# A whole-kernel list scheduler, mask copies on ScalarE and softmax sums on VectorE in a cross-attention and windowed-attention network

## The chip, the cores and the metric

The kernel runs on one NeuronCore of a Trainium2 chip. The core has TensorE (PE, matrix products), VectorE (DVE), ScalarE (ACT), GpSimd (POOL) and SyncE (SP, which issues most DMAs). Each engine works through its own queue in order; semaphores make one wait for another. The metric is the time of one execution on the device, in microseconds (us), as the median of several runs. Less is better.

## The reference

The input x has 32 batch elements of 128 tokens with 128 features, in float32. First comes one cross attention to a context of the same shape (16 query heads, 4 key heads of width 8, a time bias, a mask), then six layers of windowed self attention and feed forward:

```python
x = x + xattn(layernorm(x), ctx, ctx, deltas, mask, Wq, Wk, Wv, Wo, tw)
y = layernorm(x)
for i in range(6):
    s = shift_tokens(y)                      # second half of the features: one token later
    q, k, v = split(s @ Wqkv[i], 3)          # 16 heads of width 64
    q, k = l2norm(q) * qs, l2norm(k) * ksc   # then rotary tables cos, sin and a scale
    sim = 8 * q @ k.T                        # windows of 32: each looks at itself and the one before
    y = softmax(masked(sim)) @ v @ Wo[i] + y
    s = layer_norm(shift_tokens(y)) * g + bln
    a, gate = split(s @ W1[i] + b1[i], 2)    # 341 + 341 columns
    y = (a * gelu(gate)) @ W2[i] + b2[i] + y
return x + y
```

## The kernel before

The work unit of the layers is one batch element of one layer: 6 x 32 = 192 units. Four units are a group (`GB`), which shares the input transposes (`ax`, `axh`, `axl`) and the feed forward. Cross attention likewise has 32 units in 8 groups, each with one softmax per key head (`attn_ops`).

A layer unit goes through these steps. `qk` projects queries and keys, four PSUM banks of 512 columns, each as three products of high and low float32r parts (`split3`). Of each bank, ScalarE takes the squares (`sq`), VectorE sums them per head (`ss`) and multiplies the bank with two rotary tables (`ta` and `tb`, line 694), and GpSimd adds the two halves (`add`). The reciprocal norms of all 32 heads come as Ln, then Exp with scale -0.5 on ScalarE, refined by one Newton step on VectorE (`rsqrt_a`, `rsqrt_b`, `rsqrt_c`, lines 116 to 137). GpSimd multiplies them in (`mul`), TensorE transposes (`tq`), and ScalarE copies queries and keys out of PSUM (`ev`, `ew`); one of the four half copies of keys is done by VectorE (line 744). `y` projects the values already multiplied with Wo, ScalarE copies them out (`yt`), and 16 DMAs regroup their windows (`dm`).

Scores are taken in two halves of eight heads. In each, a bfloat16 matmul of an identity with the mask (line 781) fills the bank, and the score matmuls add to it; VectorE takes the row maxima (`mx`); ScalarE takes eight exponentials of 64 columns, each with the sum of its row as an accumulator output (`ex`, line 804), which the profile shows as a second instruction, ACTIVATION_READ_ACCUMULATOR; then reciprocal (`rl`), product on GpSimd (`pl`), a 32x32 transpose on VectorE (`PT`) and the products with the values (`av`).

At the end of a group come residual and feed forward: `res`; one DMA of 127 rows that shifts half of the features by one token (`psh`); the statistics, their Ln and Exp; then `gate`, three Gelus (`gel`), `pa`, `um`, `w2`, `res2`. ScalarE evaluates functions from a table set that has to be loaded. The compiler puts a load where the set at hand lacks the function. The kernel itself asks for the set `natural_log_exp_and_others` at the start (line 140) and behind the last Gelu of each group (line 912).

The order on every engine is written out by hand: the tables `OFF1`, `GOFF1`, `OFF` and `GOFF` give each step of each unit a place in time, `push` puts it in a heap, and `drain` emits all in the order of these times. Buffers come from rotating pools. PSUM has five banks for projections, transposes and the like (`pj`), two for scores (`pscr`) and one for attention outputs (`pou`).

Of the kernel before, what the change touches and what calls it, by code (L numbers as in the profile page):

```python
# [16 lines left out]
P = 128  # L17
# [5 lines left out]
NRT = 8  # L23
NYT = 4
NKB = 3
NQT = 3
EWD = (1,)
STORE = 0.4
MP1 = [23.0 + 1.2 * i for i in range(8)]
WV1, DH1, DL1 = [20.85, 22.05], 0.15, 0.3  # L30
PREP0, PREPT = 10.0, 7.0
SHIFT = 6.0
FFT = 7.0
MP = [31.47, 31.72, 31.97, 32.22, 32.47, 32.72, 32.97, 33.22]
WV, BIAS, DH, DL = [24.4, 25.4], 16.4, 0.06, 0.14
T1 = 7.0
NI1 = 180
OFF1 = dict(
    sc=[[0, 2, 26, 28], [32, 34, 73, 75], [93, 95, 139, 141], [154, 159, 170, 172]],
    mx=[[1, 3, 27, 29], [33, 35, 74, 76], [94, 96, 140, 142], [158, 164, 171, 173]],  # L40
    sb=[[4, 5, 30, 31], [36, 37, 77, 78], [97, 98, 143, 144], [165, 168, 174, 175]],
    ex=[[39, 41, 44, 48], [99, 100, 101, 102], [151, 152, 155, 160], [187, 189, 192, 196]],
    tp=[[42, 46, 51, 55], [126, 127, 128, 129], [153, 157, 163, 167], [190, 194, 199, 203]],
    st=[[45, 50, 54, 57], [130, 132, 134, 135], [156, 162, 178, 179], [193, 198, 202, 205]],
    pa=[[49, 53, 82, 83], [131, 133, 136, 137], [161, 166, 186, 188], [197, 201, 218, 220]],
    oT=[[84], [138], [191], [223]], pb=[[145], [146], [195], [227]], rl=[[147], [148], [200], [232]],
    at=[[149], [150], [204], [236]],
)
GOFF1 = dict(
    ldc=[-101], gst=[-121, -120], gr0=[-119], gr1=[-117, -116], gr2=[-115, -114, -113], xa=[-118], xb=[-112],  # L50
    px=[-89], pxe=[-88], pcx=[-100], pce=[-99], pk=[-77], ke=[-76], kd=[-75], pq=[-74, -73, -71, -67],
    qe=[-72, -69, -65, -62], qd=[-70, -66, -63, -60], pv=[-55], vt=[-11], td=[-110], ab=[-109, -108], ln=[-4],
    mkb=[-56], tbm=[-3], p2=[238], aT=[249], pw=[265], rs=[266], hst=[267, 268], hr0=[269], hr1=[292, 296],
    hr2=[299, 301, 302], xf1=[270], xf2=[303],
)
T = 13.3
NI = 331
OFF = dict(
    qk=[[0, 1, 30, 31], [79, 80, 107, 108], [153, 154, 194, 195], [244, 245, 284, 285]],
    sq=[[2, 6, 32, 36], [81, 85, 109, 113], [155, 159, 196, 200], [246, 250, 286, 290]],  # L60
    ss=[[7, 11, 37, 41], [86, 90, 114, 118], [160, 164, 201, 205], [251, 255, 291, 295]],
    ta=[[3, 8, 33, 38], [82, 87, 110, 115], [156, 161, 197, 202], [247, 252, 287, 292]],
    tb=[[4, 9, 34, 39], [83, 88, 111, 116], [157, 162, 198, 203], [248, 253, 288, 293]],
    add=[[5, 10, 35, 40], [84, 89, 112, 117], [158, 163, 199, 204], [249, 254, 289, 294]],
    rs0=[[42], [119], [206], [296]], rs1=[[62, 63], [141, 142], [219, 220], [313, 314]],
    rs2=[[64, 65, 66], [143, 144, 145], [221, 222, 223], [315, 316, 317]],
    mul=[[67, 68, 69, 70], [146, 147, 148, 149], [224, 225, 226, 227], [318, 319, 320, 321]],
    tq=[[100, 102, 104, 136], [181, 183, 185, 228], [268, 270, 272, 275], [354, 356, 358, 381]],
    ev=[[101, 103, 105, 137], [182, 184, 186, 229], [269, 271, 273, 276], [355, 357, 359, 382]],
    ew=[[106, 138], [187, 230], [274, 277], [360, 383]],  # L70
    y=[[127, 128, 131, 150], [235, 236, 239, 281], [304, 305, 308, 328], [374, 375, 376, 407]],
    yt=[[129, 132, 134, 151], [237, 240, 242, 282], [306, 309, 311, 329], [384, 386, 388, 408]],
    dm=[[130, 133, 135, 152], [238, 241, 243, 283], [307, 310, 312, 330], [385, 387, 389, 409]],
    sc=[[124, 125, 178, 179], [216, 217, 260, 261], [301, 302, 347, 348], [390, 391, 426, 427]],
    mx=[[126, 180], [218, 262], [303, 349], [392, 428]],
    ex=[[165, 166, 212, 213], [256, 257, 297, 298], [343, 344, 377, 378], [422, 423, 451, 452]],
    rl=[[167, 214], [258, 299], [345, 379], [424, 453]], pl=[[168, 215], [259, 300], [346, 380], [425, 454]],
    PT=[[231, 232], [322, 323], [402, 403], [470, 471]], av=[[263, 264], [350, 351], [429, 430], [506, 507]],
)
GOFF = dict(  # L80
    ax=[-53], axh=[-52], axl=[-51], res=[508], psh=[564], fst=[565, 596], xn1p=[598], frs0=[597], frs1=[655, 656],
    frs2=[657, 658, 683], xn2p=[684], ptn=[735], xnh=[736], xnl=[737], gate=[831, 832, 833], gel=[834, 835, 836],
    pa=[850, 851, 853], um=[852, 854, 855], w2=[869, 870, 871, 872], res2=[873],
)

@with_exitstack
def body(ctx: ExitStack, tc: tile.TileContext, x, ctx_in, fside, mask, xWq, xWk, xWv, xWo, xtw,
# [5 lines left out]
    NG = B // GB  # L93
    HC = [(0, 128), (128, 128), (256, HID - 256)]
    RT = HC[2][1]

    const = ctx.enter_context(tc.tile_pool(name="const", bufs=1))
    small = ctx.enter_context(tc.tile_pool(name="small", bufs=4))

    nC = cst.shape[1] - 512  # L100
    cs = const.tile([P, nC], F32, tag="cs", name="cs")
# [5 lines left out]
    shift = cs[:, 516:644]  # L107
    identb = const.tile([P, P], BF16, tag="identb", name="identb")
    nc.vector.tensor_copy(identb, ident)
    maskb = const.tile([P, 512], BF16, tag="maskb", name="maskb")  # L110
    xt = const.tile([P, B, P], F32, tag="xt", name="xt")

    def rsqrt_a(src, n, eps, floor, tagp):
        v = small.tile([P, n], F32, tag=tagp + "v", name=tagp + "v")
        if eps is not None:
            nc.vector.tensor_scalar(v, src, eps, None, op0=ALU.add)
        else:
            nc.vector.tensor_scalar(v, src, floor, None, op0=ALU.max)  # L118
        y = small.tile([P, n], F32, tag=tagp + "y", name=tagp + "y")
        t = small.tile([P, n], F32, tag=tagp + "t", name=tagp + "t")  # L120
        return v, y, t

    def rsqrt_b(a, c):
        v, y, t = a
        if c == 0:
            nc.scalar.activation(y, v, AF.Ln)
        else:
            nc.scalar.activation(y, y, AF.Exp, scale=-0.5)

    def rsqrt_c(a, c):  # L130
        v, y, t = a
        if c == 0:
            nc.vector.tensor_tensor(t, y, y, op=ALU.mult)
        elif c == 1:
            nc.vector.scalar_tensor_tensor(t, v, -0.5, t, op0=ALU.mult, op1=ALU.mult)
        else:
            nc.vector.scalar_tensor_tensor(y, t, 1.5, y, op0=ALU.add, op1=ALU.mult)  # L137
        return y

    nc.scalar.preload_act_table_set("natural_log_exp_and_others")  # L140

    wch = ctx.enter_context(tc.tile_pool(name="wch", bufs=1))
    wst = ctx.enter_context(tc.tile_pool(name="wst", bufs=1))
    pj = ctx.enter_context(tc.tile_pool(name="pj", bufs=5, space=PSUM))
    pscr = ctx.enter_context(tc.tile_pool(name="pscr", bufs=2, space=PSUM))
    pou = ctx.enter_context(tc.tile_pool(name="pou", bufs=1, space=PSUM))

    heap = []
    seq = [0]

    def push(t, fn, a):
        heapq.heappush(heap, (t, seq[0], fn, a))
        seq[0] += 1

    def drain():
        while heap:
            _, _, fn, a = heapq.heappop(heap)
            fn(*a)

    NU = NG * GB  # L160
    ws = [None] * (L + 1)

    def prep_ops(l):
        w = ws[l] = {"qk": [None] * 4, "m": [None] * 4}
        wqk = Wqkv[l]
        V = {}

        def ld(i):
            if i == 0:
                V["w1r"] = wst.tile([P, 2 * HID], F32, tag="stg", name="w1r", bufs=2)  # L170
                nc.sync.dma_start(V["w1r"], W1[l])
            elif i == 1:
                V["col"] = wst.tile([P, 2], F32, tag="lgb", name="lgb")
                nc.sync.dma_start(V["col"][:, 0:1], ln_g[l].unsqueeze(1))
            elif i == 2:
                nc.sync.dma_start(V["col"][:, 1:2], ln_b[l].unsqueeze(1))
            elif i == 3:
                w["b1"] = wch.tile([P, 2, 3], F32, tag="b1c", name="b1c", bufs=2)
                nc.vector.memset(w["b1"], 0.0)
                for s in range(2):  # L180
                    nc.sync.dma_start(w["b1"][:, s, 0:2],
                                      b1[l, s * HID:s * HID + 2 * P].rearrange("(i p) -> p i", p=P))
# [69 lines left out]
        def wve(c):  # L252
            if c == 0:
                V["wvT"] = wst.tile([P, 8, P], F32, tag="stg", name="wvT", bufs=2)
# [781 lines left out]
```

## Time and profile before

| | us |
|---|---|
| median of 3 runs | 3326.27 |
| lowest, highest | 3325.03, 3327.11 |
| span of the profiled execution | 3320.9 |

The span runs from the first to the last instruction of the profiled execution; the device time holds a little around it. These groups of the page are of use below. Each has line, engine, operation, tile written and tiles read, shapes, and count; then busy time in us and the mean length of one in ns; then the idle time of the engine just before them and what ended most of it.

```profile
L700 POOL TENSOR_TENSOR rt<-t,t 128x512 f32<-128x512 f32 x768 | 980.3, 1286 | 372.8 <-DVE t L694 330.8
L694 DVE TENSOR_TENSOR t<-pqk,tab 128x512 f32<-128x512 f32 x1536 | 983.3, 681 | 115.9 <-ACT sq L686 110.3
L804 ACT ACTIVATE pr<-sc,mx 128x64 f32<-128x64 f32 x3072 | 915.7, 331 | 61.2 <-DVE PT L817 53.0
L804 ACT ACTIVATION_READ_ACCUMULATOR pr<-sc,mx 128x1 f32 x3072 | 691.9, 225 | 0.0
L689 DVE TENSOR_REDUCE ss<-sq 128x8 f32<-128x512 f32 x768 | 517.4, 674 | 0.0
```

The lengths of neighbours overlap: an instruction may start before the end of the one ahead of it on the same engine. So the time that an instruction takes up is better read from its start to the next start, in a timeline.

### The profile page before, as it was taken

To read this page: it belongs to the slowest core of one execution; us is meant where nothing else is said; L and a number is where in the kernel's file an instruction comes from. 1 tells how busy PE (TensorE), PEld (TensorE's weight loads), DVE (VectorE), ACT (ScalarE), POOL (GpSimd) and SP (SyncE) were. 2 spreads that over 40 slices of the span, in tenths; PEclk is the share of its full clock that TensorE was granted. 3 is DMA by queue.
4 is the path that set the end of the run, shared out by engine and by line. 5 is a ranking of instruction groups with operands and counts; after the bars stand their busy time and mean duration, and the time that the engine had idled before them with its cause. 6 is when DMAs were issued, how large, how long until landed. Compare 5 with 4: busy or idle time off the path is not lost.

```text
span 3320.9 us, 102077 instructions
## 1 busy us (share of the span) xinstructions
PE 3155.8 (95%) x35979; PEld 2389.3 (72%) x35979; DVE 2979.5 (90%) x6954; ACT 2834.9 (85%) x9983; POOL 2468.3 (74%) x2284
## 2 busy tenths in 40 slices
PE   8999899999999999999999999999999999999997
PEld 5555677777777777777777777777777777777775
DVE  6666899999999999999999998998999998999995
ACT  6776888898888898889898889898888898898895
POOL 5655777777787777787787787786787776777873
PEclk9999999999999999999999999999999999999998
DMA  2110333332333332233332333332333332333332
GB/s 61 33 37 12 77 87 82 79 74 71 75 83 86 78 74 72 72 85 84 77 77 71 75 83 81 79 77 68 79 83 76 84 76 64 77 82 81 82 83 62
DMA packets 217966, 243.80 MB, mean 73 GB/s; under 512 B 83534, under 2 KB 112498, under 8 KB 217458
## 3 DMA queue, kind: packets, MB, share of 16 engines
q1 hardware_dynamic: 217026, 236.93, 28.8%
q8 instruction: 288, 4.72, 0.6%
q14 instruction: 220, 1.80, 0.2%
q10 hardware_dynamic: 432, 0.34, 0.0%
HBM read 25.31 MB, written 4.19 MB: 9 GB/s over the span
## 4 chain that ended last, share of the span: by engine, by line
PE 49%; DVE 32%; ACT 8%; issue 4%; DMA 3%; SPq 2%; POOL 1%; ACTq 0%; DVEq 0%; POOLq 0%
DVE t L694 10%; PE pO L830 8%; PE ptq L729 7%; DVE ss L689 6%; PE sc L786 4%; DVE rnv L118 3%; PE pa L542 3%; PE pqk L636 3%; PE pqk L638 3%; ACT pr L804 3%; PE pqk L637 3%; DVE mx L793 2%; DVE PT L817 2%; SPq L769 2%; PE py L636 2%
## 5 line engine op out<-in xcount | busy, mean ns | idle before, releaser
L700 POOL TENSOR_TENSOR rt<-t,t 128x512 f32<-128x512 f32 x768 | 980.3, 1286 | 372.8 <-DVE t L694 330.8
L694 DVE TENSOR_TENSOR t<-pqk,tab 128x512 f32<-128x512 f32 x1536 | 983.3, 681 | 115.9 <-ACT sq L686 110.3
L804 ACT ACTIVATE pr<-sc,mx 128x64 f32<-128x64 f32 x3072 | 915.7, 331 | 61.2 <-DVE PT L817 53.0
L723 POOL TENSOR_TENSOR rt<-rt,rny 128x512 f32<-128x512 f32 x768 | 777.4, 1043 | 214.1 <-DVE rny L137 213.4
L804 ACT ACTIVATION_READ_ACCUMULATOR pr<-sc,mx 128x1 f32 x3072 | 691.9, 225 | 0.0
L689 DVE TENSOR_REDUCE ss<-sq 128x8 f32<-128x512 f32 x768 | 517.4, 674 | 0.0
L830 PE MATMUL pO<-ysh,PT 128*32 128x128 f32 x10752 | 416.9, 275 | 53.3 <-DVE PT L817 48.7
L813 POOL TENSOR_TENSOR pr<-pr,rl 128x512 f32<-128x512 f32 x384 | 400.8, 1044 | 89.2 <-DVE rl L809 89.2
L686 ACT ACTIVATE sq<-pqk 128x512 f32<-128x512 f32 x768 | 429.3, 600 | 24.6 <-PE pqk L638 12.5
L830 PEld LDWEIGHTS pO<-ysh,PT 128*32 128x32 f32 x10752 | 367.1, 110 | 97.6 <-DVE PT L817 72.1
L762 ACT COPY yt<-py 128x512 f32<-128x512 f32 x768 | 416.8, 614 | 21.2 <-PE py L638 17.2
L729 PE MATMUL ptq<-cs,rt 128*128 128x128 f32 x3072 | 409.8, 278 | 22.2 <-DVE t L694 17.0
L729 PEld LDWEIGHTS ptq<-cs,rt 128*128 128x128 f32 x3072 | 334.5, 141 | 96.7 <-issue 52.5
L786 PE MATMUL sc<-kb,qT 128*32 128x128 f32 (+1 forms) x12288 | 375.1, 262 | 15.2 <-DVE kb L744 14.8
L786 PEld LDWEIGHTS sc<-kb,qT 128*32 128x32 f32 x12288 | 270.7, 109 | 114.5 <-issue 70.7
L636 PE MATMUL py<-mw,xsh 128*128 128x512 f32 x768 | 333.1, 434 | 8.9 <-ACT yt L762 5.8
L636 PE MATMUL pqk<-wqh,xsh 128*128 128x512 f32 x768 | 314.0, 409 | 4.8 <-ACT yt L762 2.8
L638 PE MATMUL py<-mw,xsl 128*128 128x512 f32 x768 | 301.9, 393 | 0.0
L638 PE MATMUL pqk<-wqh,xsl 128*128 128x512 f32 x768 | 300.9, 392 | 0.0
L637 PE MATMUL pqk<-wql,xsh 128*128 128x512 f32 x768 | 300.8, 392 | 0.0
L637 PE MATMUL py<-mw,xsh 128*128 128x512 f32 x768 | 300.6, 391 | 0.0
L735 ACT COPY qT<-ptq 128x512 f32<-128x512 f32 x384 | 208.1, 590 | 79.0 <-PE ptq L729 78.1
(168 smaller groups left out, 5756.8 us busy)
## 6 DMA issues: line engine op xcount, KB each, us to landing
ysh<-yt SPq DMA_DIRECT2D x3072, 64.0 KB
raw<-in_L_ffn_Wqkv SPq DMA_DIRECT2D x36, 256.0 KB
xsu<-xt SPq DMA_DIRECT2D x48, 127.0 KB
wor<-in_L_ffn_Wo SPq DMA_DIRECT2D x6, 512.0 KB
xt<-in_x SPq DMA_DIRECT2D x8, 256.0 KB
cx<-in_ctx SPq DMA_DIRECT2D x8, 256.0 KB
mk<-in_mask_BxS_ff SPq DMA_DIRECT2D x8, 256.0 KB
x_scratch<-xt SPq DMA_DIRECT2D x8, 256.0 KB
```

The lines of the kernel that those rows point to most:

```text
L636: nc.tensor.matmul(pt, lh, rh, start=True, stop=False)
L637: nc.tensor.matmul(pt, lh, rl, start=False, stop=False)
L638: nc.tensor.matmul(pt, ll, rh, start=False, stop=True)
L686: nc.scalar.activation(V["sq", c], V["pp", c], AF.Square)
L689: nc.vector.tensor_reduce(V["ss"][:, c * 8:(c + 1) * 8], V["sq", c].rearrange("p (h d) -> p h d", d=64), axis=AX.X, op=ALU.add)
L694: nc.vector.tensor_tensor(V["t", k, c].rearrange("p h s d -> p h (s d)"), V["pp", c].rearrange("p (h d) -> p h d", d=64), w["tab"][:, c // ...
L700: nc.gpsimd.tensor_tensor(V["rt", c], V["t", 0, c], V["t", 1, c][:, :, ::-1, :], op=ALU.add)
L723: nc.gpsimd.tensor_tensor(rv, rv, V["rn"][:, c * 8:(c + 1) * 8].unsqueeze(2).to_broadcast([P, 8, 64]), op=ALU.mult)
L729: nc.tensor.transpose(V["ptq", c][:, k, :], V["rt", c][:, 2 * k:2 * k + 2].rearrange("p h s d -> p (h s d)"), ident)
L786: nc.tensor.matmul(sc[32 * c:32 * c + 32, :, wd, lo:64], qT[:, c, 32 * wd:32 * wd + 32], kT[:, c, :, 32 * wd - 32 + lo:32 * wd + 32], star ...
L804: nc.scalar.activation(pr[:, q, :], scv[:, q, :], AF.Exp, bias=mx[:, q:q + 1], accum_out=ls[:, q:q + 1])
L830: nc.tensor.matmul(pO[32 * wd:32 * wd + 32, j, :], PT[:, half, wd, blk, :], ysh[u][:, (2 * par + half) * P:(2 * par + half + 1) * P], star ...
```

## The change

The hand-written orders go. A class `Sched` takes every step of the whole kernel as an operation with an engine, a time it occupies the engine and a time until its result is there (the table `COST`), a priority (the place of its unit, moved by `LATER`), the buffers it reads and writes, and for some a table, "E" or "G". `run` then plays all engines forward and gives each free engine its first ready operation in order of priority for which buffers are free. What comes out is again a fixed order on each engine. A switch between "E" and "G" counts as 1.3 us more in the plan. Ln, both kinds of Exp and the softmax Exp are all "E"; Gelu is "G".

The steps change too:

- ScalarE copies the mask into the score bank (`msk`), in place of the matmul. There is one score bank, and `pj` has six.
- The exponentials keep their eight pieces per half, in two operations of four, without the accumulator output; VectorE sums the rows (`sm`).
- Both table products are one VectorE instruction over 1024 columns (`tab`).
- All Newton steps are on GpSimd (`newton`), five instructions where VectorE had four.
- ScalarE does all four half copies of keys (`evk`).
- x is kept with its shifted half beside it, in 192 columns. The shift is done after both residuals, each time as two DMAs, of 112 and of 15 rows; the input transposes, statistics and normalisations then read 128 adjoining columns.
- The explicit load of the table set behind the Gelus is gone; the one at the start stays.

```diff
@@ softmax of half a unit
-                nc.tensor.matmul(sc.rearrange("p a b c -> p (a b c)"), identb, maskb, start=True, stop=True)
+                S.op("msk", lambda: nc.scalar.copy(sc.t, mask), pri, (), [sc], also=[pr])
...
-                nc.scalar.activation(pr[:, q, :], scv[:, q, :], AF.Exp, bias=mx[:, q:q + 1],
-                                     accum_out=ls[:, q:q + 1])
+                        nc.scalar.activation(pr.t[:, k * 64:(k + 1) * 64], sc.t[:, k * 64:(k + 1) * 64], AF.Exp,
+                                             bias=mx.t[:, k:k + 1])
+                for i in range(2):
+                    S.op("ex", lambda i=i: ex(i), pri, [sc, mx], [pr], table="E")
+                S.op("sm", lambda: nc.vector.tensor_reduce(sm.t, r8(pr), axis=AX.X, op=ALU.add), pri, [pr], [sm])
@@ reciprocal norms
-    def rsqrt_c(a, c):
...
-            nc.vector.tensor_tensor(t, y, y, op=ALU.mult)
...
-            nc.vector.scalar_tensor_tensor(t, v, -0.5, t, op0=ALU.mult, op1=ALU.mult)
...
-            nc.vector.scalar_tensor_tensor(y, t, 1.5, y, op0=ALU.add, op1=ALU.mult)
+        def f3():
+            nc.gpsimd.tensor_tensor(sl(t), sl(y), sl(y), op=ALU.mult)
...
+        S.op(names[1], f1, pri, [v], [y], table="E")
+        S.op(names[2], f2, pri, [y], [y], table="E")
+        S.op(names[3], f3, pri, [y], [t])
@@ Gelu of a group
             nc.scalar.activation(t[0:n], G["pg", i][0:n], AF.Gelu, bias=w["b1"][0:n, 1, i:i + 1])
-            if i == 2:
-                nc.scalar.preload_act_table_set("natural_log_exp_and_others")
+            S.op("gel", lambda: nc.scalar.activation(u.t[0:n], pg.t[0:n], AF.Gelu, bias=b1c.t[0:n, 1, i:i + 1]), pri,
+                 [pg, b1c], [u], table="G")
@@ the scheduler, at the choice of an operation
+                for o in cand[e]:
+                    if o.ready > t + 1e-9:
+                        continue
+                    if o.table and o.table != table and hold:
+                        continue
...
+                if o.table and o.table != table:
+                    table = o.table
+                    occ += 1.3
+                    if table == "G":
+                        hold = 3
@@ rotary products, and the shift
-            nc.vector.tensor_tensor(V["t", k, c].rearrange("p h s d -> p h (s d)"),
-                                    V["pp", c].rearrange("p (h d) -> p h d", d=64),
-                                    w["tab"][:, c // 2, k, :].unsqueeze(1).to_broadcast([P, 8, 64]), op=ALU.mult)
+            S.op("tab", lambda: nc.vector.tensor_tensor(
+                t.t.rearrange("p (k h d) -> p k h d", k=2, d=64),
+                pp.t.rearrange("p (h d) -> p h d", d=64).unsqueeze(1).to_broadcast([P, 2, 8, 64]),
+                tab.t[:, c // 2].unsqueeze(2).to_broadcast([P, 2, 8, 64]), op=ALU.mult), pri, [pp, tab], [t])
...
-            nc.sync.dma_start(xsu[1:P], xg[0:P - 1, :, 64:128])
+            nc.sync.dma_start(xt[g][1:113, :, 128:192], xt[g][0:112, :, 0:64])
+            nc.sync.dma_start(xt[g][113:P, :, 128:192], xt[g][112:P - 1, :, 0:64])
```

## The prediction

> **What bounds the kernel now.** I read the page's busy times first, then the busy times by stage, then the waits.
>
> ```profile
> PE 3155.8 (95%) x35979; PEld 2389.3 (72%) x35979; DVE 2979.5 (90%) x6954; ACT 2834.9 (85%) x9983; POOL 2468.3 (74%) x2284
> ```
>
> ```profile
> core 0: us, PE busy (x) PEld busy (x) DVE busy (x) ACT busy (x) POOL busy (x), PEclk, DMA share, GB/s
> 0.00:240.00 240.00, 219.29 (x1369) 128.98 (x1369) 158.61 (x1046) 166.10 (x334) 136.78 (x141) 0.99 0.16 45
> 240.00:300.00 60.00, 57.50 (x367) 33.97 (x366) 38.84 (x258) 40.21 (x83) 31.18 (x30) 1.00 0.03 10
> ...
> 1320.00:1830.00 510.00, 491.57 (x5858) 381.30 (x5859) 476.26 (x959) 452.37 (x1642) 391.51 (x360) 1.00 0.32 77
> ...
> 3240.00:3321.00 81.00, 56.17 (x614) 43.77 (x612) 40.73 (x93) 42.05 (x158) 31.18 (x30) 0.85 0.24 59
> ```
>
> Two stages are seen: some 300 us of cross attention, then the layers. In the layers (the 1320 to 1830 row) VectorE is busy for 476.3 of 510 us, 93.4%; ScalarE for 452.4, 88.7%. TensorE's 491.6 is no measure: its matmul ends are modelled, and records overlap (a 128x512 matmul lasts 0.39 us, but in the timeline of a stretch at 1500 us the next starts 0.23 us later).
>
> ```profile
> POOL rt L700 <- DVE t L694: 330.8, 294, 5.8
> POOL rt L723 <- DVE rny L137: 213.4, 191, 3.6
> DVE t L694 <- ACT sq L686: 110.3, 146, 5.0
> ACT rny L126 <- DVE rnv L118: 102.8, 122, 1.8
> ```
>
> The longest waits of GpSimd and a long one of ScalarE end on VectorE. So **VectorE sets the pace of the layers now**, ScalarE is five points behind, and even the leading engine loses 6.6% to waits.
>
> **The part that decides: ScalarE's table loads.** The timeline of ScalarE alone (start, length):
>
> ```profile
> 1507.19 0.32 ACT L804 ACTIVATE pr<-sc,mx 128x64 f32<-128x64 f32 x1
> 1507.39 0.22 ACT L804 ACTIVATION_READ_ACCUMULATOR pr<-sc,mx 128x1 f32 x1
> 1507.48 0.33 ACT L804 ACTIVATE pr<-sc,mx 128x64 f32<-128x64 f32 x1
> ...
> 1508.25 0.24 ACT L804 ACTIVATION_READ_ACCUMULATOR pr<-sc,mx 128x1 f32 x1
> 1508.51 1.28 ACT L910 ACT_TABLE_LOAD   x1
> 1509.81 1.83 ACT L910 ACTIVATE u<-pg,b1c 128x512 f32<-128x512 f32 x3
> 1511.65 1.28 ACT L912 ACT_TABLE_LOAD   x1
> 1512.95 1.07 ACT L735 COPY qT<-ptq 128x512 f32<-128x512 f32 x2
> ```
>
> A load holds ScalarE for 1.30 us from start to start (1508.51 to 1509.81; 1511.65 to 1512.95). Before, there are 97: one at the start, one ahead of each group's Gelus, and the explicit one behind them (L912), which brings the set with both Ln and Exp back. The change keeps only the first explicit load. Its scheduler calls Ln and Exp one table, "E", and counts a switch only between E and "G" (Gelu); but nothing tells the compiler which set to take after a Gelu. The built order of ScalarE's instructions, which has no times, shows what it takes:
>
> ```
> Ln                  223 loads ahead of it
> Exp, scale -0.5     203
> softmax Exp          57
> Gelu                 48
> first load            1   (together 532)
> ```
>
> Until the first Gelu (row 578 of 5312) there is none; from then on nearly every unit has one load ahead of its Ln and another ahead of the Exp behind it: two sets that evict each other. That is 532 - 97 = 435 loads more, 435 x 1.295 = **+563 us of ScalarE**.
>
> Two rules of the Trainium skill, "ScalarE: Activation LUTs", bear on this. Its section on table sets says that Ln followed by Exp takes one load, since one set holds both. By that the layers would have 96 loads, as the scheduler assumes, and these 563 us would be zero. The built order decides: the set exists, but isn't chosen. Its section "What ACT_TABLE_LOAD costs" gives 1283 ns for the load, which the trace confirms (1283 mean), and about 1380 ns of drain besides, 2.66 us for a switch. By that the sum would be 435 x 2.66 = 1157 us. The trace shows no such drain: the load starts 0.02 us after the last accumulator read ends (1508.25 + 0.24), and the next instruction 0.02 us after the load ends. I take 1.295.
>
> **The rest of ScalarE.** The sums of the Exps move to VectorE. An Exp and its accumulator read take 0.29 us from Exp to Exp (1507.19 to 1507.48). Without the read, the next can start after 0.20 (1507.19 to 1507.39): 3072 x 0.093 = -286. No row has these Exps alone; if they take 0.17 instead it is 80 less, if 0.23 (the length of the 128x32 Exp of L128) 100 more. Mask copies: 384 of 128x512 at the 0.48 of other such copies (two L735 in 1.07, the second 0.48 after the first) = +184; the score bank as target is not in the trace, and even the 0.60 of an unhidden copy makes it only 230. The half of kT that VectorE copied (L744): 192 x 0.48 = +92. Sum: -286 + 184 + 92 + 563 = +553, so **2834.9 becomes 3388**. Part of the 2835 are endings of 0.1 us that the next instruction would cover in a full queue: adding every group's instructions at their start-to-start times gives about 2680 before, and 3235 after.
>
> **The other engines** are all relieved to below that.
> - VectorE loses the Newton steps (L118, L133, L135, L137 for the 32-column tile: 165 + 94 + 51 + 37 = 347 us; the groups' 4-column ones 108) and L744 (133); two table products become one of twice the width, 768 x (2 x 0.60 - 1.13), about -50, where 1.13 is two start-to-starts less one fixed part of 0.07 (at 1.20 nothing is gained); half-width statistics become full-width, about -10. It gains 384 sums, 0.59 each like L689: +228. From 2980 to about 2560.
> - GpSimd gains five small steps per Newton, 256 x 5. Its nearest row is a 128x128 memset of 0.205 us; 128x16 takes 0.12, 128x512 0.52. At 0.2: +256 (154 to 666). 2468 becomes some 2720; even 3134 is below ScalarE. What queues behind the step that waits for Ln and Exp are the products of L700 and L723, which have slack once ScalarE is late.
> - TensorE loses 384 mask matmuls (149 us in the groups by line) and 384 of 576 instructions of the input transposes, now that shifted rows are stored.
> - SP issues 160 DMAs more (192 for shifts where there were 48, 32 half loads and stores for 16) at 0.63 each (16 ysh DMAs take 10.02): +100 on some 2060. A shift waits for the residual, with ysh copies behind it, as before; SP's 38% of idle time hides it. A 127-row shift lands after 10.35 us on the last group's chain; as 112 + 15 rows it may take 2 (like ysh) to 10. I take -5, at the end alone.
> - The one score bank (two before) must turn: mask 0.6, scores 1.2, maximum 0.65, eight Exps 1.7, handovers 0.3: 4.5 us, against 8.4 that ScalarE needs per half unit (3235/384). Covered, unless orders interlock.
>
> **The sum.** ScalarE can't be full everywhere. In the first 300 us it is busy for 206 (94 idle), as attention is paced by other engines; the matmuls there are the same, and in the built order only 12 of 768 squares stand ahead of attention's last step, so the layers don't fill it. In the last 81 us it is idle for 39. So 3235 + 94 + 39 = 3368 with no wait at all in the layers, already above now. To that comes what the pacing engine loses: VectorE's 6.6% of some 2950 us, 195: 3563, less 5 for the tail: a **span of 3558**. With the short endings uncovered too (3388 instead of 3235) it would be 3711. The new order was planned for a ScalarE without these loads, so the others run ahead and its inputs are mostly there; that is why I stay at 3558. What lies around the span is 3326.3 - 3320.9 = 5 us, so about **3560**, 7% slower.
>
> **The rivals.**
> - *Loads fall into waits (faster).* Without the loads ScalarE has 2672, GpSimd paces at some 2720, and with 133 + 195 the time is about 3050. Place: the load ahead of Ln, where ScalarE waits now (L126, 102.8 us in 122 waits, 0.84 each). It decides once 276 of the 563 us are covered, 49%. Against it: 122 x 0.84 is a fifth, and ScalarE's own sum of 3235 plus 133 can't be hidden; this rival needs cheaper Exps and a fuller attention stage as well. 0.06 for faster, 0.02 for no change.
> - *Waits grow.* The order was made for other durations, and each half unit loses another 0.5 us at the score bank or behind GpSimd's Newton: 384 x 0.5 = 190, about 3750. For it: one bank, in-order queues. Against: 4.5 against 8.4 us. 0.14.
> - *The drain is real.* 435 x 1.37 more: about 4150. 0.03.
> - My forecast: 0.75.
>
> Faster by over 0.2% (about what a measurement of this kernel can tell from no change) 0.06, within that 0.02, slower 0.92. The range is 3410 (ScalarE nearly full, cheaper Exps) to 3740 (endings uncovered).
>
> **What would show it.** Right: ScalarE at 95% or more in the layers, some 532 loads of 1.28 us, VectorE near 2560, mask copies near 0.5 us start to start, waits of other engines ending on ScalarE. Wrong: fewer than 200 loads in the trace, long waits of ScalarE for VectorE or GpSimd, or VectorE still above 2900.

## The result and the profile after

| | before | after |
|---|---|---|
| median, us | 3325.65 | 3838.11 |
| lowest, highest of the kernel after | | 3830.52, 3850.62 |
| span of the profiled execution, us | 3320.9 | 3848.8 |

The ratio is 1.1545, interval 1.1523 to 1.1567: the change makes the kernel 15% slower, where 7% was forecast. The direction and its cause were forecast; the time lies 98 us above the range. The profiled execution is the longest of the four.

The page of the kernel after: busy times, the granted clock of TensorE in 40 slices, and the shares of the chain that ended last.

```profile
PE 3323.1 (86%) x35213; PEld 2344.6 (61%) x35213; DVE 2633.9 (68%) x5154; ACT 3405.0 (88%) x7922; POOL 2732.7 (71%) x3528
...
PEclk9999998999999999999999999999999999989997
...
ACT 48%; PE 27%; DVE 7%; issue 7%; DMA 4%; SPq 3%; POOL 2%; ACTq 0%; POOLq 0%; DVEq 0%
```

ScalarE has taken VectorE's place as the busiest engine, and half of the chain is on it. But 88% is little for an engine that sets the pace. The busy times by stage (columns as before) say where it is not full:

```profile
core 0: us, PE busy (x) PEld busy (x) DVE busy (x) ACT busy (x) POOL busy (x), PEclk, DMA share, GB/s
0.00:240.00 240.00, 229.42 (x1372) 138.84 (x1373) 158.94 (x1015) 171.52 (x344) 154.62 (x220) 0.98 0.20 53
240.00:300.00 60.00, 59.92 (x363) 36.79 (x363) 42.58 (x238) 42.55 (x83) 38.85 (x44) 1.00 0.08 22
...
1320.00:1830.00 510.00, 439.60 (x4864) 314.40 (x4862) 351.02 (x559) 462.46 (x1089) 366.95 (x471) 0.94 0.30 68
...
3760.00:3849.00 89.00, 58.21 (x650) 43.53 (x648) 31.51 (x65) 52.08 (x127) 30.59 (x44) 0.78 0.22 49
```

In the 1320 to 1830 row ScalarE is busy for 462.5 of 510 us, 90.7%, not the 95% that was expected; every other engine has lost share against the same row of before. The granted clock, 1.00 in the layers before, is 0.94. The largest groups of ScalarE (line, operation, count; busy us, mean ns; idle us just before):

```profile
L373 ACT ACT_TABLE_LOAD x223 | 286.1, 1283 | 3.9
L376 ACT ACT_TABLE_LOAD x203 | 260.4, 1283 | 3.6
L802 ACT COPY bank__67<-mask 128x512 f32<-128x512 f32 x384 | 235.8, 614 | 0.1
L811 ACT ACT_TABLE_LOAD x57 | 73.1, 1283 | 2.4 <-DVE mx__19814 L808 0.7
L872 ACT ACT_TABLE_LOAD x48 | 61.6, 1283 | 0.9
```

The 532 loads are there (531 in these four rows, one at the start), each 1283 ns. ScalarE's timeline in one unit shows the two table sets evicting each other:

```profile
1500.27 1.28 ACT L373 ACT_TABLE_LOAD   x1
1501.56 0.23 ACT L373 ACTIVATE ry__19654<-rv__19575 128x32 f32<-128x32 f32 x1
1501.70 0.58 ACT L736 ACTIVATE sq__19659<-bank__65 128x512 f32<-128x512 f32 x1
1502.30 1.28 ACT L376 ACT_TABLE_LOAD   x1
1503.59 0.23 ACT L376 ACTIVATE ry__19654<-ry__19654 128x32 f32<-128x32 f32 x1
...
1505.85 1.74 ACT L811 ACTIVATE pr__19621<-bank__67,mx__19691 128x64 f32<-128x64 f32 x8
```

Two loads of 1.28 us for two instructions of 0.23. The eight Exps at the end take 1.74 together, 0.196 from one to the next. The longest waits of the kernel after (engine, tile and line that waited, who ended it: us in total, times, longest) are new:

```profile
PEld bank__67 L799 <- ACT bank__67 L802: 320.4, 259, 5.0
PE bank__67 L799 <- ACT bank__67 L802: 221.4, 180, 4.5
```

TensorE stands in its queue before the scores, waiting for ScalarE to copy the mask into the one score bank, for up to 5 us at a time. In the first experiment below, which has the same order without the extra loads, the second of these rows is

```profile
PE bank__67 L799 <- ACT bank__67 L802: 77.2, 103, 3.7
```

so the loads lengthen these waits. How far they come back to ScalarE as waits of its own is left to the experiments.

### The profile page after: what moved, and what is told of

The parts are those of the page before. It is cut to its first block, busy times and chain, and to the rows that moved or that the text cites. A ratio compares the mean times of both kernels' runs of the same rounds, so it can differ in the third digit from the quotient of the medians.

```text
span 3848.8 us, 97225 instructions
## 1 busy us (share of the span) xinstructions
PE 3323.1 (86%) x35213; PEld 2344.6 (61%) x35213; DVE 2633.9 (68%) x5154; ACT 3405.0 (88%) x7922; POOL 2732.7 (71%) x3528
## 4 chain that ended last, share of the span: by engine, by line
ACT 48%; PE 27%; DVE 7%; issue 7%; DMA 4%; SPq 3%; POOL 2%; ACTq 0%; POOLq 0%; DVEq 0%
ACT L373 6%; ACT L376 5%; PE bank__67 L799 4%; ACT bank__67 L802 3%; SPq L782 3%; PE bank__68 L829 3%; ACT L811 2%; ACT kb__82 L769 1%; ACT L872 1%; ACT kb__82 L768 1%; PE bank__64 L406 1%; PE bank__62 L406 1%; PE bank__66 L406 1%; ACT kb__81 L769 1%; PE bank__65 L406 1%
## 5 line engine op out<-in xcount | busy, mean ns | idle before, releaser
L373 ACT ACT_TABLE_LOAD x223 | 286.1, 1283 | 3.9
L376 ACT ACT_TABLE_LOAD x203 | 260.4, 1283 | 3.6
L802 ACT COPY bank__67<-mask 128x512 f32<-128x512 f32 x384 | 235.8, 614 | 0.1
L811 ACT ACT_TABLE_LOAD x57 | 73.1, 1283 | 2.4 <-DVE mx__19814 L808 0.7
L872 ACT ACT_TABLE_LOAD x48 | 61.6, 1283 | 0.9
L839 DVE TENSOR_TENSOR xt<-bank__68,xt 128x512 f32<-128x512 f32 x48 | 32.5, 678 | 6.7 <-PE bank__68 L829 6.7
L768 ACT COPY kb__81<-bank__66 64x512 f32<-64x512 f32 x55 | 32.8, 596 | 3.2 <-PE bank__66 L406 3.2
L769 ACT COPY kb__81<-bank__66 64x512 f32<-64x512 f32 x55 | 32.0, 581 | 1.2
L768 ACT COPY kb__82<-bank__64 64x512 f32<-64x512 f32 x38 | 22.3, 586 | 5.0 <-PE bank__64 L406 4.9
L768 ACT COPY kb__82<-bank__66 64x512 f32<-64x512 f32 x37 | 21.9, 592 | 5.0 <-PE bank__66 L406 4.9
L768 ACT COPY kb__82<-bank__63 64x512 f32<-64x512 f32 x39 | 23.1, 592 | 2.0 <-PE bank__63 L406 1.9
L768 ACT COPY kb__82<-bank__62 64x512 f32<-64x512 f32 x38 | 22.2, 584 | 2.3 <-PE bank__62 L406 2.2
L769 ACT COPY kb__82<-bank__63 64x512 f32<-64x512 f32 x39 | 22.7, 581 | 0.9
L769 ACT COPY kb__82<-bank__62 64x512 f32<-64x512 f32 x38 | 22.1, 582 | 0.8
L769 ACT COPY kb__82<-bank__64 64x512 f32<-64x512 f32 x38 | 22.1, 581 | 0.8
L769 ACT COPY kb__82<-bank__66 64x512 f32<-64x512 f32 x37 | 21.5, 581 | 0.8
L768 ACT COPY kb__81<-bank__64 64x512 f32<-64x512 f32 x29 | 17.3, 595 | 1.9 <-PE bank__64 L406 1.9
L768 ACT COPY kb__82<-bank__61 64x512 f32<-64x512 f32 x29 | 17.0, 588 | 1.5 <-PE bank__61 L406 1.5
L768 ACT COPY kb__81<-bank__61 64x512 f32<-64x512 f32 x27 | 16.1, 597 | 2.4 <-PE bank__61 L406 2.4
L769 ACT COPY kb__81<-bank__62 64x512 f32<-64x512 f32 x29 | 16.9, 581 | 0.6
L769 ACT COPY kb__82<-bank__61 64x512 f32<-64x512 f32 x29 | 16.9, 581 | 0.6
L769 ACT COPY kb__81<-bank__64 64x512 f32<-64x512 f32 x29 | 16.9, 581 | 0.6
```

The source lines that it names most:

```text
L373: nc.scalar.activation(sl(y), sl(v), AF.Ln)
L376: nc.scalar.activation(sl(y), sl(y), AF.Exp, scale=-0.5)
L768: S.op("evk", lambda: nc.scalar.copy(d.t[0:64, :, 0, :], p3()[0:64]), pri, [pt], [d])
L769: S.op("evk", lambda: nc.scalar.copy(d.t[64:128, :, 1, :], p3()[64:128]), pri, [pt], [d])
L802: S.op("msk", lambda: nc.scalar.copy(sc.t, mask), pri, (), [sc], also=[pr])
L811: nc.scalar.activation(pr.t[:, k * 64:(k + 1) * 64], sc.t[:, k * 64:(k + 1) * 64], AF.Exp, bias=mx.t[:, k:k + 1])
```

## The experiments

Each kernel was timed in three rounds beside the kernel before, which took 3324 to 3326 us in all of them. "Loads cured" is the kernel after with one line more (first experiment). Several tables below give **ScalarE's idle time in the layers**: the gaps between its instructions from 300 us to some 89 us before the end (81 in the kernel before), worked out from the trace, each put down to the engine that ended it. Of long lines of the tables `COST` and `LATER` the cuts show only the entries that change. Where an experiment changes what the scheduler plans with (a step, a duration, a priority, a pool), all else is planned anew too; e1, e4, the i runs and j2 leave the order as it was.

The expectations pit theories against each other. Of the eighteen times only four fell into a stated range (h3, h4, i1, i2): the kernels were harder to foresee than the theories allowed, and what follows rests on the measured differences.

### Are the loads the loss? (e1_reload, e4_before_no_reload)

One kernel gives the changed kernel its explicit load back; the other takes it from the kernel before.

```diff
@@ e1_reload: the kernel after, behind each third Gelu
+                if gels[0] % 3 == 0:
+                    nc.scalar.preload_act_table_set("natural_log_exp_and_others")
@@ e4_before_no_reload: the kernel before
-            if i == 2:
-                nc.scalar.preload_act_table_set("natural_log_exp_and_others")
```

> The changed kernel with one thing put back: behind the third Gelu of each group ScalarE loads the set that has both Ln and Exp (97 loads in the built order instead of 532). Theory A, the loads are the cost, by their own time and by the waits they cause: ScalarE's busy time falls from 3405 to about 2840, the time to 3050-3200 us, below the 3326 of before. Rival B, the new order itself costs the time (one score bank, mask copies in ScalarE's queue, TensorE waiting for them): the loads' own 563 us at most come off and most of the waits stay, 3350-3500 us.

> The kernel before, with its explicit load behind the Gelus taken out and nothing else: 553 loads in the built order instead of 97, 456 x 1.295 = 591 us more ScalarE. Theory A: ScalarE becomes the pacing engine there too, 2835 + 591 = 3426 busy, and with 133 us of ends and 200-350 of waits in the layers 3760-3910 us. Rival B: the hand-written order has room for them in ScalarE's 486 us of idle time: 3330-3500 us.

Measured: e1_reload **3291.64 us**, ratio 0.9897 (0.9883 to 0.9912); e4_before_no_reload 3718.84, ratio 1.1183 (1.1166 to 1.1199). In the trace of e1_reload the only loads left, beside the first, are

```profile
L873 ACT ACT_TABLE_LOAD x48 | 61.6, 1283 | 0.9
L876 ACT ACT_TABLE_LOAD x48 | 61.6, 1283 | 0.8
```

So the loads are the whole loss, and more: without them the change gains 1.0%, and this kernel beats both. 435 loads at 1.295 us are 563 us, and taking them away gives 546: 97% of them lay on the path. In the kernel before, 456 loads more are 591 us, and cost 394: 67%. Loads of the same kind are hidden to a third by one order and hardly at all by the other. Both times fell between the ranges of theories A and B. Where the difference lies, ScalarE's idle time tells:

| kernel | layers, us | ScalarE busy | idle | ended by TensorE | ended by VectorE |
|---|---|---|---|---|---|
| before | 2940 | 2587 | 354 | 167 | 157 |
| before, without its load (e4) | 3326 | 3131 | 195 | 128 | 6 |
| after, loads cured (e1) | 2901 | 2566 | 335 | 181 | 101 |
| after | 3460 | 3139 | 321 | 186 | 97 |

The windows view of the layers as a whole, e4_before_no_reload first and the kernel after second, carries the busy column:

```profile
300.00:3626.00 3326.00, 2908.05 (x33622) 2213.32 (x33621) 2719.04 (x5558) 3131.22 (x9850) 2271.13 (x2083) 0.98 0.28 68
```

```profile
300.00:3760.00 3460.00, 2975.53 (x32833) 2125.42 (x32832) 2400.84 (x3837) 3138.81 (x7371) 2508.67 (x3221) 0.94 0.29 67
```

ScalarE has the same work in both, 3131 and 3139 us, yet the layers take 134 us longer in the second. In the order by hand, loads fell into ScalarE's waits for VectorE, which went from 157 us to 6: the forecast's picture of an engine whose inputs lie ready. In the planned order ScalarE's waits stay nearly whole (335 and 321) when the loads come on top. Another difference in these rows is TensorE's granted clock, 0.98 and 0.94. No run separates its part in the 134 us (see the last section).

### Does a plan that knows the loads wait less? (e3_plan_knows)

The scheduler is told that Ln and Exp have tables of their own once a Gelu has run, 1.3 us for each switch. The loads stay (521).

```diff
-        S.op(names[1], f1, pri, [v], [y], table="E")
+        S.op(names[1], f1, pri, [v], [y], table="L")
...
-                if o.table and o.table != table:
-                    table = o.table
+                if o.table and o.table != table and (gelu or o.table == "G"):
+                    table, gelu = o.table, True
```

> The changed kernel, whose scheduler is told that after the first Gelu Ln and Exp are two tables and that each switch takes ScalarE 1.3 us; the built order has 521 loads, nearly as many. If the 321 us that ScalarE waits in the layers come from an order planned for other durations: 3600-3700 us. If loads in an in-order queue cost these waits however they are planned: 3780-3860 us.

Measured: 3721.34 us, ratio 1.1188 (1.1169 to 1.1207), 117 us less than the kernel after. ScalarE is busy for 3389.5 us instead of 3405.0; its idle time in the layers falls from 321 to 216. The time lies between the two ranges. A plan that knows the loads thus waits a third less, and what is left is near the 195 that the forecast had put there. That the knowledge is the cause isn't shown, for any other plan is another order: h1_joined below knows nothing of the loads, and its ScalarE waits 220 us.

### The mask: back to TensorE (e2_mask_on_pe, g3_reload_mask_pe)

```diff
-                S.op("msk", lambda: nc.scalar.copy(sc.t, mask), pri, (), [sc], also=[pr])
+                S.op("msk", lambda: nc.tensor.matmul(sc.t, identb, maskb, start=True, stop=True), pri, (), [sc], also=[pr])
...
-    msk=("ACT", .49, .60)
+    msk=("PE", .32, .45)
```

> The changed kernel with the mask back on TensorE (bfloat16 matmul, as before), all else and the loads (538) as changed. Theory A: ScalarE loses 236 us of copies and stays the pacing engine, at about 3170 busy plus waits: 3550-3650 us. Rival B, TensorE's 540 us of waiting for the mask copy are what lengthens it: 3300-3400 us.

> The explicit load put back (97 loads), one score bank, and the mask on TensorE. ScalarE loses some 235 us of busy time. If ScalarE paces without the loads too: 3080-3180 us. If waits between engines pace it, as taking the copies out of the changed kernel gave only 45 us: 3220-3280 us.

Measured: 3793.08 (ratio 1.1407, 1.139 to 1.1424), 45 us less than the kernel after, though ScalarE has 171 us less to do; with loads cured 3337.16 (1.0033, 1.0022 to 1.0045), 46 us more than e1_reload. ScalarE's idle time rises from 321 to 429 and from 335 to 542. Both times lie above both ranges. The copy on ScalarE never waits for its bank (idle before it: 0.1 us in 384, in the row above), since the Exps that free the bank stand ahead of it in the same queue. As a matmul it waits for them in TensorE's queue. But that isn't why the kernels don't gain: TensorE's idle time at this place in the layers, whatever ended it, falls from 220 us before the scores to 193 before the mask, and with loads cured from 74 to 46. Why ScalarE waits longer stays open. In these plans the mask is better off on ScalarE with loads cured, and its 0.6 us there cost less than they seem to.

### The score bank (g1_two_banks, g2_reload_two_banks, g4_reload_mask_pe_two; h1 to h4)

From the trace, the time from one freeing of the score bank to the next, as means in the layers of the kernel after: 0.5 us to the mask copy, 0.6 the copy, 0.4 to the scores, 2.2 scores, 1.0 to the maximum, 0.7 maximum, 1.5 to the Exps, 2.2 Exps: 9.2 us. The forecast had 4.5, "against 8.4 that ScalarE needs". The sum alone says little: with one bank, 384 turns follow one another and fill the layers, whatever sets the pace (3460 us / 384 = 9.0). What the pieces tell is that 3.4 us of the turn are waits between steps, where the forecast had 0.3. Such a bank could set the pace, so it was given a partner from the six banks of the projections:

```diff
-    S.pool("pj", bank[0:6], False)
+    S.pool("pj", bank[0:5], False)
...
-    S.pool("sc", bank[6:7])
+    S.pool("sc", bank[5:7])
```

> The changed kernel with two score banks and five for projections (as before the change), loads as changed (527). Theory C: with one bank the next half's mask copy and scores can't start until this half's Exps are done, TensorE stands at them in its in-order queue, and the loads lengthen each turn of the bank; with two banks these waits (542 us of TensorE on the mask copy) mostly go and the time falls to 3550-3700 us. Rival: the copy's place in ScalarE's queue is what counts, not the bank: 3780-3850 us.

> The explicit load behind the Gelus put back (97 loads) and two score banks. If the one bank is why the kernel without the extra loads takes 3292 us and not the 3050 that its engines' sums allow: 3120-3220 us. If not: 3260-3320 us.

> All three: the explicit load (97 loads), the mask on TensorE, and two score banks. No engine is then over 2750 us busy by the profile but TensorE, whose busy time is modelled. Theory: 3030-3150 us, the fastest of all. Rival, waits elsewhere (GpSimd's Newton steps, in-order queues) hold it: 3200-3300 us.

Measured: 3976.32 (ratio 1.1953, 1.1934 to 1.1971), 3538.07 (1.0632, 1.0611 to 1.0653) and 3589.53 (1.0803, 1.0779 to 1.0826): slower by 138, 246 and 252 us than the same kernels with one score bank. In these plans the sixth projection bank is worth far more than a second score bank. That may be no property of the banks, since the numbers of banks that the plan keeps free (`KEEP`) were left as they were for six; so it doesn't settle the turn either.

So the turn was shortened in place: scores in one step and Exps in one step (h1, h2), or both earlier in priority (h3), or both (h4). The joined steps got their longer durations in `COST` too.

```diff
@@ h1, h2, h4
-                S.op("sc0", lambda: scores(0), pri, [q, k, sc], [sc])
-                S.op("sc1", lambda: scores(1), pri, [q, k, sc], [sc])
+                S.op("sc0", lambda: (scores(0), scores(1)), pri, [q, k, sc], [sc])
...
-                for i in range(2):
-                    S.op("ex", lambda i=i: ex(i), pri, [sc, mx], [pr], table="E")
+                S.op("ex", ex, pri, [sc, mx], [pr], table="E")
@@ h3, h4: LATER
-    sc0=0.75, ex=2
+    sc0=-0.5, ex=-0.5
```

> The changed kernel, loads as changed (532), with the two halves of the scores as one step and the eight Exps as one step, so that nothing comes between them. Theory D, the turn of the one score bank (9.16 us in the trace) sets the pace: the scores take 1.3 us instead of 2.2 and the Exps 1.75 instead of 2.2, the turn falls by 0.7-1.3 us, the time by 250-500: 3350-3600 us. Rival E, the projection banks and their emptying set it: 3780-3880 us.

> The same with the explicit load put back (97 loads). Theory D: 3000-3150 us, against 3292 without the joining. Rival E: 3260-3330 us.

> The explicit load put back, steps as changed, but scores and Exps are moved ahead in the order of priority (from 0.75 and 2 units later than their own unit to half a unit earlier). Theory D: the turn falls below 7.2 us and the time to 3050-3200 us. Rival E: 3270-3350 us.

> Load put back, joined steps, and these first in priority. Theory D: as fast as the faster of the two or faster, 2980-3150 us. Rival E: 3260-3350 us.

| kernel | loads | us | ratio (interval) | turn, us |
|---|---|---|---|---|
| h1_joined | 532 | 3753.69 | 1.1288 (1.1272 to 1.1305) | 8.9 |
| h2_reload_joined | 97 | 3335.02 | 1.0033 (1.0021 to 1.0045) | 7.8 |
| h3_reload_first | 97 | 3340.66 | 1.0047 (1.0032 to 1.0062) | 7.8 |
| h4_reload_joined_first | 97 | 3332.33 | 1.0020 (1.0013 to 1.0028) | 7.8 |

With the loads cured the steps of the turn don't set the pace: joined scores take 1.0 us instead of 2.0 and joined Exps 1.75 instead of 2.2, but the handovers grow by as much, the turn stays where it was (7.6 in e1_reload), and the time rises by 41 to 49 us. With the loads, joining gives 84 us, and ScalarE's idle time falls from 321 to 220, as in e3; whether the joined steps or merely the other order did it was not separated.

### Which engine holds the cured kernel? (i1 to i4, j1, j2)

Since VectorE had 365 us less to do in e1_reload than before, a gain of only 34 asks for another limit. TensorE's matmul row is at 95% there:

```profile
PE 3127.8 (95%) x35213; PEld 2249.7 (68%) x35213; DVE 2614.6 (79%) x5154; ACT 2827.6 (86%) x7487; POOL 2730.0 (83%) x3528
```

i1 (from e1_reload), i2 (from the kernel before) and i4 (from the kernel after) leave out the third product of `qk`, high part of the weights by low part of x. i3 leaves the Newton step of the query and key norms out of the kernel before, on VectorE.

```diff
@@ i1, i2, i4 (after's form)
-            S.op("qk", lambda: split3(pp.t, (xh.t[:, j, :], xl.t[:, j, :]), (hi.t, lo.t)), pri, [xh, xl, hi, lo], [pp],
+            S.op("qk", lambda: split2(pp.t, xh.t[:, j, :], (hi.t, lo.t)), pri, [xh, xl, hi, lo], [pp],
@@ i3
-            V["rn"] = rsqrt_c(V["rsq"], c)
+            V["rn"] = V["rsq"][1]
```

> The kernel with the explicit load put back (97 loads, 3292 us), without the third of the three products of every query and key projection (low part of x times high part of the weights); the order is the same. TensorE loses 768 matmuls of 0.23 us, 177 us; no other engine changes. Theory F, TensorE paces: 3115-3180 us. Rival G, waits spread over four engines: 3240-3300 us.

> The kernel before, without the same third product. F, TensorE paced it, not VectorE: 3150-3220 us. If VectorE paced it, as the prediction had it: 3290-3330 us.

> The kernel before, without the Newton step on the reciprocal norms of queries and keys (three VectorE instructions per unit, 182 us busy and fewer waits behind ScalarE); the Ln and Exp stay. If VectorE paced: 3130-3200 us. F: 3280-3330 us.

> The changed kernel with its 532 loads, without the third product as above. If with the loads ScalarE's queue alone paces: 3800-3840 us. If the loads stand in a chain that runs through TensorE too: 3690-3770 us.

| kernel | us | ratio (interval) | against | work taken off (page's busy time) | time |
|---|---|---|---|---|---|
| i1_reload_two | 3272.12 | 0.9841 (0.9827 to 0.9856) | e1_reload | TensorE 135 | -20 |
| i2_before_two | 3312.03 | 0.9960 (0.9946 to 0.9975) | before | TensorE 186 | -13 |
| i3_before_no_newton | 3242.93 | 0.9750 (0.9733 to 0.9766) | before | VectorE 137 | -82 |
| i4_after_two | 3869.24 | 1.1631 (1.1614 to 1.1649) | after | TensorE 110 | +31 |

The page of i3 shows what its VectorE was relieved of (2979.5 us in the kernel before):

```profile
PE 3067.4 (94%) x35645; PEld 2365.3 (73%) x35979; DVE 2842.3 (88%) x6378; ACT 2820.5 (87%) x9983; POOL 2463.1 (76%) x2284
```

The 186 of i2 are too many, as some 300 records of its products are missing; 768 products at 0.23 us are 177. TensorE doesn't hold the cured kernel or the kernel before, for all its 95%; i4 came out slower, outside both ranges. The Trainium skill ("Trainium Kernel Development and Optimization", "Performance Expectations") warns that matmul busy time is a bad metric for how close a kernel is to the chip's limit, because matmuls are pipelined, and points to the weight loads' busy share, among others (68% in e1_reload); these runs agree on the first. VectorE did hold the kernel before, for the most part: 60% of what it was relieved of came through (82 us of 137, between the two ranges), though this edit also shortens the way from Exp to the products on GpSimd.

GpSimd had been given VectorE's Newton steps. In e1_reload, j1 moves all five instructions back to VectorE (known to the plan); j2 lets the four refining ones emit nothing and keeps the order.

```diff
@@ j1
-            nc.gpsimd.tensor_tensor(sl(t), sl(y), sl(y), op=ALU.mult)
+            nc.vector.tensor_tensor(sl(t), sl(y), sl(y), op=ALU.mult)
@@ j2
-        S.op(names[3], f3, pri, [y], [t])
+        S.op(names[3], none, pri, [y], [t])
```

> The changed kernel with the explicit load behind each third Gelu (97 loads), and all five Newton instructions on VectorE in place of GpSimd, known to the scheduler. VectorE was busy for 2615 us with these loads and GpSimd for 2730; this moves some 250 us from GpSimd to VectorE, so about 2870 and 2480. Theory H (GpSimd took over as the pace when it was given the Newton steps): the time falls from 3292 to 3200 or less. Theory G (waits spread over in-order engines, no one of them paces): within 30 us of 3292, and slower rather than faster, since the full share only moves from one engine to another.

> The changed kernel with the explicit load behind each third Gelu, and the four refining instructions of each Newton step left out, so that the reciprocal norms are the unrefined Exp; the order of all else is kept as planned with them. GpSimd loses 256 x 4 small steps, about 210 us of 2730, and the way from Exp to the products of GpSimd gets 0.8 us shorter in each unit. Theory H (GpSimd paces): the time falls by 100 us or more, to below 3190. Theory G: by 10 to 50 us, as with the third product left out on TensorE.

Measured: j1 3391.02 (1.0202, 1.0185 to 1.0219), j2 3292.26 (0.9901, 0.9886 to 0.9915). Their busy times, j1 first:

```profile
PE 3138.0 (93%) x35213; PEld 2262.3 (67%) x35213; DVE 2998.6 (88%) x6434; ACT 2834.6 (84%) x7487; POOL 2458.8 (73%) x2248
```

```profile
PE 3122.4 (95%) x35213; PEld 2248.9 (68%) x35213; DVE 2613.8 (79%) x5154; ACT 2827.2 (86%) x7487; POOL 2517.1 (76%) x2504
```

In j2 GpSimd has 213 us less to do and a unit's chain is four steps shorter, and the time doesn't move by a microsecond: theory H falls. (Theory G had asked for 10 to 50 us, so its number missed too.) In j1 VectorE gets 384 us back in a plan made anew, and it costs 99, which neither H nor G had foreseen. At VectorE's old load the changed kernel with its loads cured is thus 66 us slower than the kernel before (3391 against 3325), and relieving VectorE gains 99. **Put together: 3325 + 66 - 99 + 546 = 3838.** The sum closes by itself, since each term is the step from one measured kernel to the next; what it shows is the size of the steps. Of these only the 546 is one line with the order kept. The 99 has a new plan in it, and the 66 all else that the change does.

What holds e1_reload at 3292 stays open. Relief of TensorE gave 20 us and of GpSimd none, VectorE (79% busy) was not relieved further, and ScalarE's could only be had by giving work to TensorE, which cost 46. ScalarE's idle 335 us are spread over waits for TensorE's value projections (75), its query and key projections (42), VectorE's rotary products (52) and row maxima (44), and smaller ones. That they form rings through queues in fixed order is the reading that is left; no run isolated such a ring.

## Why the prediction was right in kind and wrong in size

**Right.** The changed kernel takes 532 loads, 1.283 us long and 1.295 from start to start, without a drain; the two sets evict each other; ScalarE becomes the busiest engine and other engines' longest waits end on it. The Exps come every 0.196 us (0.20 forecast); ScalarE's busy time is 3405 (3388), GpSimd's 2733 (2720), VectorE's 2634 (2560). ScalarE's idle time at the two ends is 86 and 37 us (94 and 39). Rival one fell: 3% of the loads' time was covered. (By its own figures 51% would have had to be: from 3050 to 3326 there is room for 276 us of loads, so these 276, 49%, are what could stay uncovered.) Rival three, the drain, fell.

**Wrong: the waits, and the choice of 3235.** The forecast's span was 3558 = 3235 + 94 + 39 + 195 - 5. The trace has 3849 = 3405 busy + 86 + 37 idle at the ends + 321 idle in the layers. The 291 us between them:

| term of the sum | forecast | measured | difference |
|---|---|---|---|
| ScalarE's own time | 3235 | 3405 | +170 |
| waits in the layers | 195 | 321 | +126 |
| ends | 133 | 123 | -10 |
| earlier tail | -5 | 0 | +5 |

The step that failed is the last but one sentence of the sum: "The new order was planned for a ScalarE without these loads, so the others run ahead and its inputs are mostly there; that is why I stay at 3558." It decided both terms, the 195 and the choice of 3235 over 3388. What the runs showed in its place: in the order planned without the loads the others did not run ahead. ScalarE kept nearly all its waits (321, where the cured kernel has 335), and the loads came on top at 97%. In the order by hand, with as many loads, its waits are 195: the forecast's number was, by chance, that of the *other* order. With the loads in the plan they are 216 (e3). How the others fell behind is a reading of the waits: TensorE stands at the scores until ScalarE, late by its loads, has copied the mask (212 us of its idle time in the layers), and the projections behind it in the same queue, for which ScalarE waits in turn (93 us at `yt`; 75 in the cured kernel), come later by that. No run isolated this ring, and TensorE's slower clock is a second candidate.

Of the 170, 153 are the choice of 3235: with the endings left uncovered the forecast's own sum was 3388, and 17 are missing to 3405. The choice assumed a queue so full that each instruction's end is covered by the next. Counting each group at its median from start to start, and at most at its length, ScalarE's instructions come to 2747 us in the kernel before and 3295 in the kernel after; the busy times are 88 and 110 more, so the endings are covered no better than before. Inside the sum of 553 the mask copy was mis-sized: its median from start to start is 0.607 us, not 0.48, and 384 x 0.127 is 49; the forecast had named 0.60 as its upper end. Other terms together took 32 off.

"Waits grow" was the rival nearest to the truth (3750), with the right place, the score bank. Its price was too small because the bank's turn was reckoned at 4.5 us from bare durations: its four handovers, each a place in somebody's queue, take 3.4 us in the trace instead of 0.3, and scores and Exps, each in two steps with other work between, 2.2 instead of 1.2 and 1.7. But shorter steps did not shorten the turn of the cured kernel, so there it is a sign of these waits rather than their cause. The same error stood in rival one, which put the kernel without the loads at "about 3050"; it takes 3292. A busy sum plus a fixed share of waits was 242 us too low there, where no run found one engine that sets the pace.

## What to carry to other kernels

Before a kernel's order is replaced by a planned one, ask whether each duration in the plan is one that the compiled program will show: a hidden instruction on the busiest engine was paid nearly in full here, in an order that was made without it. In fixed queues the lateness of one engine can become waits of the engines that feed it; take the waits of the new order from runs of the new order, not from the share that the old one lost. Where Ln, Exp and another function share an engine, count the table loads in the built program, and ask for the shared set explicitly.

## What the runs showed of the hardware

**TensorE's clock falls with its waits.** The granted clock drops to half in steps of 3.413 us: for 7 us of the layers before, 34 in e1_reload, 133 in e4_before_no_reload, 420 in the kernel after, 539 in i4_after_two. In the layers of the kernel after, divided into such steps, all 52 steps at full clock in which TensorE's products were busy for less than 40% were followed by half clock, 40 of the 140 between 40 and 70%, and none of the 778 above. The timeline of TensorE in the kernel after shows one such stretch (in brackets the idle time before):

```profile
1502.90 0.40 PE L402 MATMUL bank__65<-wch__11423,xl__19188 128*128 128x512 f32 x1
1506.02 1.11 PE L406 MATMUL bank__64<-cs,sq__19614 128*128 128x128 f32 x4 [2.72 <-POOL sq__19614 L856]
...
1510.49 0.63 PE L401 MATMUL bank__66<-nl__19731,w1h__4601 128*128 128x512 f32 x1
1510.92 0.63 PE L402 MATMUL bank__66<-nh__19730,w1l__4653 128*128 128x512 f32 x1
...
1512.74 0.39 PE L401 MATMUL bank__62<-nl__19731,w1h__4601 128*85 128x512 f32 x1
```

After a wait of 2.72 us the products take 0.43 us from start to start, and 0.23 again from 1512.5 on. The Trainium skill ("TensorE: Matmul & The Clock Gate", "What's actually happening") tells of half rate after an idle window of about 3.4 us; the steps agree, but here the window ahead of the half rate (1502.1 to 1505.5 in the clock's records) was idle only for its last 2.2 us. So a TensorE that waits more runs slower when its inputs come. In the kernel after, products are busy for 388 of the 420 us at half clock, in e1_reload for 31 of 34. At half the rate that is an estimated 194 us of TensorE's time at most, against 15. How much of the kernel after's 126 us of extra waits comes from it was not isolated. Nor does it explain i4_after_two by itself: by the same estimate the clock costs that kernel 51 us more than the kernel after, less than the 110 us that its busy TensorE time fell by with this included, and yet it is 31 us slower.

**What a copy costs depends on what stands behind it.** ScalarE's 128x512 mask copy from SBUF into the bank takes 0.607 us from start to start, its copies of the same shape out of PSUM 0.48. Little of that is the bank as target. Behind it, in 162 of 384 cases, stands L769, the copy of a half of the keys on partitions 64 to 127; and all 384 of these start 11 to 27 ns after the instruction ahead has ended, so its end is never covered. Ahead of an L769 the mask copy takes 0.638 us and a copy out of PSUM (L780) 0.636. Ahead of L768, the half on partitions 0 to 63, they take 0.520 and 0.482. In h1_joined, where L769 follows only 48 of the mask copies, their median is 0.52.

**Products of one kind in a row are cheaper.** A product of 512 columns follows the first of its three by 0.23 us where the one ahead was of the same kind, by 0.32 to 0.34 where it was another. The order by hand has 1360 of 1824 such products behind another product, the planned one 734.
